# A 3x3 depthwise convolution as matmuls: its taps in 64-row or 64-column tiles, two halves of the tokens side by side

## Chip, core and metric

One core of a Trainium2 chip runs the whole program in one launch. The metric is the time of one execution on the device, in microseconds (us). About 0.2% of this kernel's time, 38 us, is what a measurement can tell from no change.

## What is computed

The input is four images of 64x64 tokens with 96 channels, in float32. Four layers are applied one after the other. Each layer adds a token mixer and then a feed-forward network (with 8-bit and 16-bit rounding) to the tokens. The mixer of layer 0 is a gated linear recurrence along the tokens. The mixers of layers 1 to 3 are two-dimensional selective scans over 192 inner channels. Ahead of each scan stands a depthwise 3x3 convolution, the part that is changed here:

```python
xz = x @ in_proj_w.T
xi, z = jnp.split(xz, 2, axis=-1)
xc = jnp.transpose(xi, (0, 3, 1, 2))
xc = jax.lax.conv_general_dilated(xc, conv_w, (1, 1), 'SAME', feature_group_count=Di) + conv_b[None, :, None, None]
xc = jax.nn.silu(xc)
```

Depthwise means that each of the 192 channels (`Di`) is convolved with nine weights of its own. The result `u` then runs through four directional scans of 4096 steps with 16 states for each channel.

## The kernel before

**Stages.** `gated` (line 1034) does layer 0 for the four images. Its work comes in 384 tiles of 512 tokens (4 images, 8 strips of 512 tokens, 12 groups of states). For each tile TensorE (PE) makes two projections into the wide PSUM tile `bc` and one into `c`. VectorE (DVE) turns them into a decay `da` and an input, and runs the recurrence as one scan instruction into `h`. GpSimd (POOL) multiplies `h` by `c`, and every third tile PE adds three products up into `sum`. `scans` (line 839) then does the twelve selective scans (three layers, four images) as 4608 tiles of 1024 tokens, 384 for each stage. In each tile ScalarE (ACT) computes `da`, PE broadcasts a row into the wide PSUM tile `bc` (`b_rows`, line 883), DVE multiplies (`bc<-du,bc`) and scans (`h<-da,carry,bc`), POOL multiplies by `c`, and PE adds the result into `acc` (`add_quarters`, line 919). `add_quarters` already issues its matmuls as four tiles of 64 rows by 64 columns, with `tile_position`.

**Between the stages.** All that lies between two scans of one image is written as Python generators: the previous mixer's end, the feed-forward network, the next layer's input projection and the convolution (`between`, line 623). A `Job` (line 717) advances them. It earns a number of steps with every tile (1.6 during the scans, 2.6 in layer 0 and for the last images), and at each step every live generator goes on to its next `yield`. So the number of `yield`s in a generator sets over how many tiles its work is spread. The convolution of image 0 ahead of layer 1 runs while layer 0 works on the images after it. The eleven others run during the scans.

**Order of the work.** `InOrder` (line 68) ties each engine's instructions to the order in which the program issues them. All of them are issued through one helper line, so the profile calls nearly every instruction L78, and groups are told apart by their tiles. On PE the order within a tile of the scans is the broadcast for the next tile, then the job's matmuls, then the accumulation of a tile that was scanned earlier. A matmul of the job thus stands ahead of the next broadcast.

**PSUM.** Two banks of 512 float32 columns serve all the job's matmuls (`x_proj`, `dt_proj`, `in_proj`, `conv` and others). `bank` (line 125) takes one and `release` gives it back at the end of the tile. `yield True` lets a generator go on only when a bank is free.

**The convolution.** `project_in` (line 511) leaves a strip of 8 image rows by 64 with a border in the SBUF tiles `pad0` and `pad1`. `pad0` holds channels 0 to 127. `pad1` holds channels 128 to 191 twice, in its upper 64 partitions shifted by one image row. `convolve` (line 570) multiplies shifted views of these by diagonal matrices, one for each tap, which `derive_taps` (line 300) makes once for each layer: nine of 128x128 for `pad0` (`tap_lo`) and six for `pad1` (`tap_hi`). The first three of the six handle two image rows at once over 128 partitions, and the last three use 64 partitions. Each group accumulates in one bank, which one ACT copy of 128x512 takes out to `u`. After that come the bias, the Silu and the stores. There are 96 strips in all (3 layers, 4 images, 8 strips), so 96 x 15 taps.

Of the kernel before, what the change touches and what calls it, by code (L numbers as in the profile page):

```python
# [14 lines left out]
AF = mybir.ActivationFunctionType  # L15
# [3 lines left out]
HW = 64  # L19
# [7 lines left out]
MM = 512  # L27
G = MM // 128
NSTRIP = L // MM
SR = MM // HW  # L30
# [12 lines left out]
W_CW = W_OUT + 2 * C  # L43
# [56 lines left out]
def metaformer(ctx: ExitStack, tc: tile.TileContext, x, l0_ab, l0_rest, ssm, ffn, out):  # L100
    nc = tc.nc
    pe, act, dve, pool, sp = (
        InOrder(tc, e) for e in (nc.tensor, nc.scalar, nc.vector, nc.gpsimd, nc.sync)
    )
# [6 lines left out]
    def sb(bufs, tag, shape, dtype=F32):  # L111
        return pools[bufs].tile(shape, dtype, tag=tag, name=tag)

    def const(name, shape, dtype=F32):
        return pools[1].tile(shape, dtype, name=name)
# [7 lines left out]
    banks = {"free": 2, "back": 0, "pool": pbc}  # L123

    def bank(name):
        banks["free"] -= 1
        return banks["pool"].tile([128, MM], F32, tag="ps", name=name)

    def release():
        banks["back"] += 1  # L130
# [28 lines left out]
    ident = const("ident", [128, 128])  # L159
    make_identity(nc, ident)  # L160
    twice = const("twice", [128, 128])
    for k in range(2):
        p = slice(64 * k, 64 * k + 64)
        dve.tensor_copy(twice[p, 0:64], ident[p, p])
        dve.tensor_copy(twice[p, 64:128], ident[p, p])
    stacked = twice[:, 0:64]
# [6 lines left out]
    for n in range(NS):  # L173
        for k in range(2):
            at = NS * k + n
# [101 lines left out]
    class Weights:  # L277
# [22 lines left out]
        def derive_taps(self, some):  # L300

            if 0 in some:
                self.lo = sb(1, "tap_lo", [128, 9, 128])
                self.hi = sb(1, "tap_hi", [128, 6, 128])
            for t in some:
                src, dst = (ident, self.lo[:, t, :]) if t < 9 else (twice, self.hi[:, t - 9, :])
                act.activation(dst, src, AF.Copy, scale=self.w[:, W_CW + t : W_CW + t + 1])

    weights = {}

# [109 lines left out]
    def measure_x(im, s, hold):  # L420

        x1 = load_x(im, s)
        yield
        yield
        norm = Norm()
        yield from norm.measure(x1, C, 1e-5)
        hold["x", s] = x1, norm
# [131 lines left out]
    def gate_z(im, s, hold):  # L559
        if s < NSTRIP:  # L560
            for z in hold["z"][s]:
                act.activation(z, z, AF.Silu)
# [7 lines left out]
    def convolve(im, layer, s, hold):  # L570

        lo, hi = hold["pads"].pop(s)
        taps = weights[layer]
        w = taps.w
        raw = []
        groups = (
            [(taps.lo[:, t, :], lo[:, t // 3 : t // 3 + SR, t % 3 : t % 3 + HW]) for t in range(9)],
            [(taps.hi[:, t, :], hi[:, 0:SR, t : t + HW]) for t in range(3)]
            + [(taps.hi[0:64, 3 + t, :], hi[0:64, 2 : 2 + SR, t : t + HW]) for t in range(3)],
        )  # L580
        for i, group in enumerate(groups):
            ps = bank("conv")
            for at, (lhs, rhs) in enumerate(group):
                pe.matmul(ps, lhs, rhs, start=at == 0, stop=at == len(group) - 1)
                yield
            v = sb(1, f"u{i}", [128, MM])
            act.copy(v, ps)
            release()
            yield i == 0
            raw.append(v)  # L590
        for i, v in enumerate(raw):
            act.activation(v, v, AF.Silu, bias=w[:, W_CB + i : W_CB + i + 1])
        gate_z(im, s + 1, hold)
        yield
        yield
        store_z(im, s + 1, hold)
        t = slice(s * MM, (s + 1) * MM)
        cols_a, part_c = hold["cols"]
        sp.dma_start(out=im.u[0, 0:64, t], in_=raw[0][0:64])
        sp.dma_start(out=im.u[1, 0:64, t], in_=raw[0][64:128])  # L600
        sp.dma_start(out=im.u[2, 0:64, t], in_=raw[1][0:64])
        for p, src, dst, c0, nc_ in (
            (slice(0, 128), raw[0], cols_a, 0, HW),
            (slice(0, 64), raw[1], part_c, 0, HW // 2),
            (slice(64, 128), raw[1], part_c, HW // 2, HW // 2),
        ):
            pool.tensor_copy(
                dst[p].rearrange("p (c r) -> p r c", r=HW)[:, SR * s : SR * s + SR, :],
                src[p].rearrange("p (r c) -> p r c", c=HW)[:, :, c0 : c0 + nc_],
            )  # L610
            if p.start or p.stop == 128:
                yield
        if s == NSTRIP - 1:
            yield
            sp.dma_start(out=im.u[1, 64:128, :], in_=cols_a[0:64])
            sp.dma_start(out=im.u[0, 64:128, :], in_=cols_a[64:128])
            for k in range(2):
                sp.dma_start(
                    out=im.u[2, 64:128, k * L // 2 : (k + 1) * L // 2],
                    in_=part_c[64 * k : 64 * k + 64],  # L620
                )

    def between(im, layer, dst=None):


        hold = {"in": {}, "pads": {}, "z": {}}
        new = dram.tile([L, C], F32, tag="x", name="x") if dst is None else dst

        def columns():
            return sb(1, "cols_a", [128, L]), sb(1, "part_c", [128, L // 2])  # L630

        def first():
            if layer:
                cols_a, part_c = hold["cols"] = columns()
                sp.dma_start(out=cols_a[0:64], in_=im.y[1, 64:128, :])
                sp.dma_start(out=cols_a[64:128], in_=im.y[0, 64:128, :])
                for k in range(2):
                    sp.dma_start(
                        out=part_c[64 * k : 64 * k + 64],
                        in_=im.y[2, 64:128, k * L // 2 : (k + 1) * L // 2],  # L640
                    )
                load_y(im, 0, hold)
            for _ in range(9 if layer else 3):
                yield

        yield [Chain(first())]
        done = {"y": 0, "x": 0, "end": 0}

        def joins():
            for s in range(NSTRIP):  # L650
                yield lambda: done["x"] > s - 2
                yield True
                yield from join_orders(im, s, hold)
                done["y"] += 1

        def mixers():
            for s in range(NSTRIP):
                yield lambda: done["end"] > s - 2 and (
                    layer == 0 or (done["y"] > s and hold["y", s][1].known)
                )  # L660
                if layer:
                    yield from mixer_out(im, layer, s, hold)
                else:
                    yield from measure_x(im, s, hold)
                done["x"] += 1

        def feeds():
            for s in range(NSTRIP):
                yield lambda: done["x"] > s and hold["x", s][1].known
                yield from feed_forward(im, layer, s, hold, new)  # L670
                done["end"] += 1

        yield [Chain(f()) for f in (feeds, mixers, joins)[: 3 if layer else 2]]
        if dst is not None:
            return

        def second():
            if layer + 1 not in weights:
                weights[layer + 1] = Weights(layer + 1)
                for _ in range(4):  # L680
                    yield
                weights[layer + 1].derive()
                for t in range(0, 15, 3):
                    yield
                    weights[layer + 1].derive_taps(range(t, t + 3))
            im.x = new
            im.u = dram.tile([3, 128, L], F32, tag="u", name="u")
            im.z = dram.tile([DI, L], F32, tag="z", name="z")
            hold["cols"] = columns()
            hold["in"][0] = load_x(im, 0)  # L690
            yield
            yield

        yield [Chain(second())]
        done = {"in": 0, "out": 0}

        def takes():
            for s in range(NSTRIP):
                yield lambda: done["out"] > s - 3
                yield from take_in(im, layer + 1, s, hold)  # L700
                done["in"] += 1

        def convolves():
            yield lambda: done["in"] > 0
            gate_z(im, 0, hold)
            yield
            yield
            store_z(im, 0, hold)
            for s in range(NSTRIP):
                yield lambda: done["in"] > min(s + 1, NSTRIP - 1)  # L710
                yield True
                yield from convolve(im, layer + 1, s, hold)
                done["out"] += 1

        yield [Chain(f()) for f in (convolves, takes)]
# [557 lines left out]
    with tc.tile_pool(name="pbig", bufs=2, space=bass.MemoryType.PSUM) as wides_pool:  # L1273
# [5 lines left out]
        for at in range(len(stages)):  # L1279
            jobs.append([])  # L1280
            if at + 1 < len(stages):
                im, layer = stages[at + 1]
# [126 lines left out]
```

## Time and profile before

| what | us |
|---|---|
| median of 3 runs | 19235.74 |
| lowest and highest | 19232.23, 19267.89 |
| profiled execution, own time | 19244.18 |
| profiled execution, span from first to last instruction | 19242.4 |
| DVE busy in it | 17682.6 |
| PE busy in it | 15910.7 |
| POOL busy in it | 13533.8 |
| ACT busy in it | 11062.2 |

In the trace a float32 matmul is two PE instructions, each with a weight load: 1728 rows of `conv<-pad,tap_lo` are 96 x 9 taps, twice. PE rows include the time until a matmul's end, so consecutive rows overlap, and the distance from start to start tells what a matmul takes from PE. A DVE that is busy nearly all the time in a stretch sets the pace there, and the waits of DVE in that stretch tell what could be won. PEclk is the clock that PE was granted, as a share of the full one.

### The profile page before, as it was taken

To read this page: it belongs to the slowest core of one execution; us is meant where nothing else is said; L and a number is where in the kernel's file an instruction comes from. 1 tells how busy PE (TensorE), PEld (TensorE's weight loads), DVE (VectorE), ACT (ScalarE), POOL (GpSimd) and SP (SyncE) were. 2 spreads that over 40 slices of the span, in tenths; PEclk is the share of its full clock that TensorE was granted. 3 is DMA by queue.
4 is the path that set the end of the run, shared out by engine and by line. 5 is a ranking of instruction groups with operands and counts; after the bars stand their busy time and mean duration, and the time that the engine had idled before them with its cause. 6 is when DMAs were issued, how large, how long until landed. Compare 5 with 4: busy or idle time off the path is not lost.

```text
span 19242.4 us, 219783 instructions
## 1 busy us (share of the span) xinstructions
PE 15910.7 (83%) x69248; PEld 4675.9 (24%) x69248; DVE 17682.6 (92%) x13768; ACT 11062.2 (57%) x17831; POOL 13533.8 (70%) x9222
## 2 busy tenths in 40 slices
PE   8998787787787788788888788788888788788887
PEld 3332121121122222222222222222222222222323
DVE  6757999999999999999999999999999999999985
ACT  4544564555555665665665665665665665666664
POOL 3434777777777777777777777777777777777775
PEclk9998796786787797797797797797787787788775
DMA  2213666666676667667667677667676676676664
GB/s 52 51 45 93 167 189 170 167 187 171 167 194 176 171 186 185 172 186 183 171 187 182 174 191 182 170 187 187 168 192 180 171 192 179 170 198 176 168 180 115
DMA packets 1269846, 3192.04 MB, mean 166 GB/s; under 512 B 440336, under 2 KB 440560, under 8 KB 1262544
## 3 DMA queue, kind: packets, MB, share of 16 engines
q1 hardware_dynamic: 1268688, 3177.97, 62.7%
q8 instruction: 559, 9.16, 0.2%
q14 instruction: 599, 4.91, 0.1%
HBM read 2818.51 MB, written 308.28 MB: 162 GB/s over the span
## 4 chain that ended last, share of the span: by engine, by line
DVE 62%; PE 17%; ACT 10%; issue 4%; DMA 3%; POOL 3%; SPq 1%; DVEq 1%; POOLq 0%; ACTq 0%
DVE h L78 43%; DVE bc L78 16%; ACT da L78 5%; PE bc L78 4%; PE acc L78 4%; PE conv L78 2%; ACT L78 2%; DMA c<-cs 2%; POOL c L78 1%; PE dt_proj L78 1%; SPq L78 1%; DVE st L78 1%; PE y_t L78 1%; PE c L78 1%; POOL du L78 1%
## 5 line engine op out<-in xcount | busy, mean ns | idle before, releaser
L78 POOL TENSOR_TENSOR c<-h,c 128x1024 f32<-128x1024 f32 (+1 forms) x4992 | 11337.3, 2274 | 5052.2 <-DVE h L78 3027.9
L78 DVE TENSOR_TENSOR_SCAN h<-da,carry,bc 128x1024 f32<-128x1024 f32 x4608 | 10798.8, 2343 | 559.6 <-POOL c L78 53.5
L78 PE MATMUL acc<-c,twice 64*64 64x512 f32 x36864 | 6386.0, 770 | 35.5 <-POOL c L78 31.2
L78 ACT ACTIVATE da<-delta,decay 128x1024 f32<-128x1024 f32 x4608 | 5285.0, 1148 | 1687.0 <-DVE h L78 1680.0
L78 PE MATMUL bc<-bs,sel 96*128 96x512 bf16 x9216 | 3509.2, 470 | 2769.7 <-DVE h L78 2671.1
L78 DVE TENSOR_TENSOR bc<-du,bc 128x1024 f32<-128x1024 f32 x4608 | 5567.0, 1208 | 181.5 <-PE bc L78 170.8
L78 ACT COPY carry<-h 128x1 f32<-128x1 f32 x3456 | 652.8, 189 | 3929.1 <-DVE h L78 3924.3
L78 PEld LDWEIGHTS <-sel 96*128 96x128 bf16 x9216 | 563.8, 102 | 7896.7 <-DVE h L78 6245.7
L78 PEld LDWEIGHTS acc<-c,twice 64*64 64x64 f32 x36864 | 1149.8, 156 | 2898.8 <-issue 2020.8
L78 ACT ACT_TABLE_LOAD x1287 | 1651.2, 1283 | 37.7 <-DVE mv L78 19.8
L78 PE MATMUL conv<-pad,tap_lo 128*128 128x512 f32 x1728 | 918.7, 638 | 0.0
L78 PE MATMUL dt_proj<-rows,w 12*128 12x512 f32 x1152 | 841.3, 817 | 6.4 <-ACT delta L78 3.9
L78 ACT COPY y<-acc 128x1024 f32<-128x1024 f32 x288 | 291.6, 1012 | 808.6 <-PE acc L78 785.8
L78 PE MATMUL x_proj<-u,xp 128*108 128x512 f32 x1152 | 715.0, 739 | 20.2 <-DMA xp<-in_ssm 8.5
L78 POOL TENSOR_TENSOR du<-delta,u 128x1024 f32<-128x1024 f32 x288 | 678.9, 2357 | 1.5 <-issue 1.5
L78 ACT ACTIVATE c<-c,l_bias 128x512 f32<-128x512 f32 x384 | 263.4, 686 | 658.4 <-PE c L78 655.7
L78 PE MATMUL conv<-pad,tap_hi 128*128 128x512 f32 (+1 forms) x1152 | 606.8, 630 | 1.6 <-ACT u L78 1.6
L78 DVE TENSOR_TENSOR_SCAN h<-da,l_carry,bc 128x512 f32<-128x512 f32 x384 | 491.5, 1280 | 42.4 <-DVE bc L78 1.8
L78 PE MATMUL y_t<-ident,pad 128*128 128x128 f32 (+1 forms) x1536 | 389.2, 340 | 51.3 <-DMA pad<-y 40.6
L78 PE MATMUL bc<-rows,u 96*128 96x512 f32 x768 | 395.4, 640 | 41.6 <-DVE h L78 41.6
L78 PEld LDWEIGHTS conv<-pad,tap_lo 128*128 128x128 f32 x1728 | 339.7, 204 | 324.4 <-issue 255.1
L78 PE MATMUL bc<-xp,u 96*128 96x512 f32 x768 | 391.0, 634 | 24.2 <-DVE h L78 24.0
(143 smaller groups left out, 12353.1 us busy)
## 6 DMA issues: line engine op xcount, KB each, us to landing
c<-cs SPq DMA_DIRECT2D x9216, 256.0 KB, 4.2
u<-u SPq DMA_DIRECT2D x288, 512.0 KB, 6.7
y<-y SPq DMA_DIRECT2D x1152, 128.0 KB, 3.5
y<-y SPq DMA_DIRECT2D x144, 512.0 KB, 6.2
xr<-x SPq DMA_DIRECT2D x224, 192.0 KB, 5.0
u<-u SPq DMA_DIRECT2D x288, 128.0 KB, 3.9
pad<-y SPq DMA_DIRECT2D x288, 128.0 KB, 4.8
z<-zl SPq DMA_DIRECT2D x96, 256.0 KB, 4.5
```

What stands on the lines that cost most here:

```text
L78: ins = f(*a, **k).ins
```

## The change

The diagonal tap matrices become 64 columns wide (`stacked` holds two 64x64 identities, one above the other, so partition p holds its weight in column p mod 64), in one tile `taps` of 15.

For the first group, a tap becomes four matmuls of 64 rows by 64 columns over 256 tokens: `j` picks the upper or lower half of the channels, `k` the first or second half of the strip's tokens. The channel halves accumulate in two PSUM banks, and the token halves in the lower and upper 64 partitions of each. For the second group, a tap becomes two matmuls of 64 columns, one for each half of the tokens, in one bank. The first three use 128 rows, the last three 64.

Four ACT copies of 64x256 instead of one of 128x512 take each group out, and put the quarters where they belong in `u`. The generator yields after every second tap and once at the end of a group, where it yielded after every tap. Before a strip it waits until both banks are free, in one step where there were two.

```diff
@@ def derive_taps(self, some):
-                self.lo = sb(1, "tap_lo", [128, 9, 128])
-                self.hi = sb(1, "tap_hi", [128, 6, 128])
+                self.taps = sb(1, "taps", [128, 15, 64])
             for t in some:
-                src, dst = (ident, self.lo[:, t, :]) if t < 9 else (twice, self.hi[:, t - 9, :])
-                act.activation(dst, src, AF.Copy, scale=self.w[:, W_CW + t : W_CW + t + 1])
+                act.activation(
+                    self.taps[:, t, :], stacked, AF.Copy, scale=self.w[:, W_CW + t : W_CW + t + 1]
+                )
@@ def convolve(im, layer, s, hold):
-        for i, group in enumerate(groups):
-            ps = bank("conv")
-            for at, (lhs, rhs) in enumerate(group):
-                pe.matmul(ps, lhs, rhs, start=at == 0, stop=at == len(group) - 1)
-                yield
+        half = MM // 2
+
+        def rows(k, first):
+            return slice(first + SR // 2 * k, first + SR // 2 * (k + 1))
+
+        def tap_lo(ps, t):
+            for k in range(2):
+                for j in range(2):
+                    p = slice(64 * j, 64 * j + 64)
+                    pe.matmul(
+                        ps[j][64 * k : 64 * k + 64, 0:half],
+                        taps[p, t, :],
+                        lo[p, rows(k, t // 3), t % 3 : t % 3 + HW],
+                        start=t == 0,
+                        stop=t == 8,
+                        tile_position=(64 * j, 64 * k),
+                    )
+
+        def tap_hi(ps, t):
+            m, first = (128, 0) if t < 3 else (64, 2)
+            for k in range(2):
+                pe.matmul(
+                    ps[0][64 * k : 64 * k + 64, 0:half],
+                    taps[0:m, 9 + t, :],
+                    hi[0:m, rows(k, first), t % 3 : t % 3 + HW],
+                    start=t == 0,
+                    stop=t == 5,
+                    tile_position=(0, 64 * k),
+                )
+
+        for i, (tap, n) in enumerate(((tap_lo, 9), (tap_hi, 6))):
+            ps = [bank("conv") for _ in range(2 - i)]
+            for t in range(n):
+                tap(ps, t)
+                if t % 2:
+                    yield
+            yield
             v = sb(1, f"u{i}", [128, MM])
-            act.copy(v, ps)
-            release()
+            for j in range(2):
+                for k in range(2):
+                    act.copy(
+                        v[64 * j : 64 * j + 64, half * k : half * (k + 1)],
+                        ps[j if i == 0 else 0][64 * k : 64 * k + 64, 0:half],
+                    )
+            for _ in ps:
+                release()
             yield i == 0
...
@@ def convolves():
-                yield lambda: done["in"] > min(s + 1, NSTRIP - 1)
-                yield True
+                yield lambda: done["in"] > min(s + 1, NSTRIP - 1) and banks["free"] > 1
                 yield from convolve(im, layer + 1, s, hold)
```

More of the change, by code (lines that the diff above doesn't have):

```diff
@@ L572, in convolve @@
         lo, hi = hold["pads"].pop(s)
-        taps = weights[layer]
-        w = taps.w
+        w, taps = weights[layer].w, weights[layer].taps
         raw = []
[L576 to L580, printed above, removed]
-        for i, group in enumerate(groups):
-            ps = bank("conv")
-            for at, (lhs, rhs) in enumerate(group):
-                pe.matmul(ps, lhs, rhs, start=at == 0, stop=at == len(group) - 1)
-                yield
-            v = sb(1, f"u{i}", [128, MM])
-            act.copy(v, ps)
-            release()
+        half = MM // 2
```

## Prediction

> **What bounds the kernel now.** I first read the page's shares and slices, then the busy time in chosen windows, then what DVE waits for in them. The page:
>
> ```profile
> PE 15910.7 (83%) x69248; PEld 4675.9 (24%) x69248; DVE 17682.6 (92%) x13768; ACT 11062.2 (57%) x17831; POOL 13533.8 (70%) x9222
> ...
> DVE  6757999999999999999999999999999999999985
> ```
>
> DVE is at 0.9 or more from about 2400 us on, but not in the first five slices. There are two regimes, layer 0 and the scans. The windows view shows one line from layer 0 with feed-forward work beside it, one from layer 0 with the convolution, and one from a scan stage with the convolution (columns: window and length, then PE, PEld, DVE, ACT, POOL busy, PE clock, DMA).
>
> ```profile
> 345.00:830.00 485.00, 441.24 (x1289) 176.88 (x1290) 373.43 (x598) 257.29 (x566) 226.06 (x390) 0.95 0.21 51
> 939.00:1466.00 527.00, 487.58 (x1228) 191.57 (x1226) 287.79 (x376) 238.83 (x486) 180.21 (x330) 0.94 0.19 47
> 8244.00:8669.00 425.00, 378.13 (x1584) 107.30 (x1583) 406.66 (x239) 270.95 (x448) 317.22 (x205) 0.93 0.69 188
> ```
>
> In layer 0 with the convolution PE is busy 487.6 of 527 us (93%), DVE 55%, ACT 45%, POOL 34%: PE is the bound. In the scan stage DVE is busy 406.7 of 425 (96%). DVE's waits in the latter two windows:
>
> ```profile
> DVE da L78 <- PE bc L78: 116.0, 58, 5.3
> ```
>
> ```profile
> DVE bc L78 <- PE bc L78: 3.0, 3, 2.4
> ```
>
> So a shorter convolution is worth its full PE time in layer 0 (one of twelve convolutions of an image) and nearly nothing in the eleven others, where DVE waits 3.0 us for PE in 425. Over the eleven windows these waits are 3.7, 4.5, 5.0, 1.2, 3.0, 3.8, 0.7, 3.3, 0.4, 3.8 and 0.7: **30 us in all**.
>
> **The change part by part.**
>
> *Streaming.* What one tap takes from PE now is read from starts. In layer 0:
>
> ```profile
> 1100.07 1.91 PE L78 MATMUL conv<-pad,tap_lo 128*128 128x512 f32 x4
> ...
> 1101.81 1.88 PE L78 MATMUL bc<-rows,u 96*128 96x512 f32 x4
> 1103.53 1.02 PE L78 MATMUL c<-rows,u 96*128 96x512 f32 x2
> ```
>
> Four instructions lie 1.72 to 1.74 us apart, 0.43 us each, so a tap (two) is 0.86 us. Matmuls in four tiles of 64x64 are already in the trace:
>
> ```profile
> 17244.40 1.98 PE L78 MATMUL conv<-pad,tap_hi 64*128 64x512 f32 x4
> 17246.31 1.09 PE L78 MATMUL acc<-y,twice 64*64 64x512 f32 x8
> 17247.22 1.04 PE L78 MATMUL acc<-c,twice 64*64 64x512 f32 x8
> 17248.19 0.60 PE L78 MATMUL bc<-bs,sel 96*128 96x512 bf16 x2
> ```
>
> Eight of them, four matmuls, take 17247.22 - 17246.31 = 0.91 us, hardly more than two instructions of the full array. The four run side by side, with two banks and tile positions as in the change. A first-group tap is the same eight instructions over 256 columns: half, 0.43 us. That instructions or weight loads don't set a floor above it is shown by `y_t<-ident,part_c` (8 instructions of 64 columns): 151.9 us for 3072, 49 ns each, 8 x 49 = 0.40 us at worst, below 0.43. A second-group tap has two tiles of 64 columns over 256 tokens; its nearest row is `sum<-c,fold 128*32` (three column tiles, six instructions in some 0.86 us at 512 columns), so also half. The convolution's PE time is 918.7 + 606.8 = 1525 us on the page, 124 of it in layer 0 (14.77 and 109.18 in the windows of 500:1000 and 1000:1500). Half of it goes: **62 us in layer 0**, some 700 in the scans.
>
> *Changes of tile shape.* Above, four `conv` instructions take 1.91 us between `bc` and `acc`, against 1.74 in layer 0 among matmuls of full width: 0.17 us for a stretch between shapes. In layer 0 the neighbours are 96*128 and the stretches now cost nothing extra. In the changed program's order the convolution stands in 30 tiles of layer 0 (56 before), so 30 stretches x 0.2 to 0.3 us: **+8 us** (bounds 0 and 15). In the scans it stands between `bc` (96*128) and `acc` (64*64) already, and the first group now has `acc`'s shape; I take 0. The Trainium skill, "TensorEngine Tiling (Array Packing)", section Key Properties, says that a change of tiling mode drains TensorE. The 0.17 us agree, and it speaks against the change in layer 0; the page has no price, so the sum goes by the row.
>
> *Taking the banks out.* Two copies of 128x512 become eight of 64x256 for each strip. ACT's groups:
>
> ```profile
> L78 ACT COPY u<-conv 128x512 f32<-128x512 f32 x192 | 109.7, 571 | 50.5 <-PE conv L78 36.7 <-POOL c L78 9.4 <-issue 3.8
> L78 ACT COPY yt<-y_t 128x384 f32<-128x384 f32 x192 | 89.4, 466 | 132.4 <-PE y_t L78 131.2
> ```
>
> 128 columns are worth 0.105 us, so 256 columns are 0.466 - 0.105 = 0.36 us. Eight are 2.89 against 1.14: +1.75 us for a strip, 168 us of ACT time over 96 strips, in fours of 1.44 us. Queued behind them on ACT are the next `carry` and `da`. `da` is issued two tiles (7.2 us) ahead of its scan, and ACT is busy 271 of 425 us in the scan window, 1.3 us free in each tile of 3.6. So I cost it at nothing. In layer 0 the cover is ACT's 55% of idle time. The same page's section PSUM Bottleneck warns that tiling speeds up the matmuls but not the copies; the rows agree (2.5 times the ACT time), but they lie beside DVE or PE.
>
> *Banks and yields.* The first group holds both banks, so `dt_proj` and `x_proj` may have to wait for one. In the changed order all but a few `dt_proj` stand in the same tiles of their item, none later than the eighth of 16 (its result is needed at the next item), and layer 0's preparation ends by the eighth of twelve tiles, where it ended by the seventh. Cost 0. There are nine yields for 15 taps instead of 15. A step now carries two taps of 0.43 us where it carried one of 0.86: the PE load of a tile stays the same, and the convolution is over in half as many tiles (464 for 880 in the scans). The jobs end some ten tiles earlier, with 50 to 90 tiles of each stage free of them already: no gain. ACT's table loads go from 1287 to 1289 (2.6 us, hidden). `derive_taps` saves 45 x 0.05 us on ACT: nothing.
>
> *Scans.* Half of the 30 us of waits goes with half of the tiles, -15; eviction and bank waits may give some back. I take **-10** (bounds -30 and +30). POOL and DMA do the same work. What is late next is DVE itself.
>
> *The sum*, on the profiled execution's own 19244.2 us: -62 + 8 in layer 0, -10 in the scans = -64, so 19180. The median of the runs is 8.4 us under that execution: 19235.7 - 64 = **19172**.
>
> **Bounds for layer 0.** Upper: the tiles of the convolution's window take 527/96 = 5.49 us, those of 345:830 take 485/120 = 4.04. If half of this difference went, 96 x 1.45 / 2 = 70. Lower: if only half of PE's saving shows, because ACT, POOL and DVE in turn hold a tile back, (62 - 8)/2 = 27.
>
> **The rivals.**
>
> 1. *As forecast*: 19172, from 19115 (70 in layer 0, 30 in the scans, 20 for the spread of runs) to 19197 (-38). Chance 0.71.
> 2. *The pace of layer 0 passes to another chain.* There `POOL c <- ACT c` waits are long, and DVE waits for `sum`. Against it: the window without convolution has PE at 91% with tiles of 4.04 us, so PE sets the pace there as well. It would give -27 in layer 0 and 0 in the scans: 19209. Chance 0.17.
> 3. *The change doesn't do what it says*: the two column tiles of one row half don't stream side by side over short pieces, and a tap stays 0.86 us. For it: no 256-column piece is in the trace. Against: `acc` and `part_c`. It gives +8 in layer 0: 19244. Chance 0.04.
> 4. *Slower: the copies come to the path.* Place: ACT in the scans' convolution windows. Price: 88 strips x 1.75 = 154 us there, less 54 in layer 0: +100, 19336. It decides once ACT runs more than the 7.2 us behind that `da` has. Against it: DVE waits for `da` 0.5 us at most in any of the eleven windows. Chance 0.08.
>
> **How the numbers follow.** About 0.2%, 38 us, is what a measurement can tell from no change. Rival 1 lies beyond it: faster 0.71. Rivals 2 and 3 lie within: same 0.21. Rival 4: slower 0.08. The range for 8 in 10 takes in rival 1 and most of rival 2: 19115 to 19215.
>
> **What would show it.** In the profile after, the eight instructions of a first-group tap should take about 0.43 us from start to start of the next tap, with the `conv` groups about 760 us less busy on PE; the tiles of layer 0 with convolution should take some 4.9 us instead of 5.5, and layer 0 should end some 55 us earlier; the scan stages should keep 3.6 to 3.7 us a tile. I am wrong if `conv` matmuls of one tap don't start within some ns of each other, if DVE waits for `da` in the scans' convolution windows, if the granted clock there falls well below 0.92 and waits for `bc` grow, or if layer 0's tiles stay at 5.5 with PE less busy.

## The result and the profile after

The changed kernel takes **19337.01 us** (median of 4 runs, 19331.18 to 19363.0) against 19242.88 for the kernel before in the same series: a ratio of 1.0050, interval 1.0032 to 1.0067. It is 94 us slower, where 64 us faster was forecast. The profiled execution took 19363.0 us with a span of 19361.2; it was the slowest of the four, so its difference to the profile before, 119 us, is somewhat more than the medians'. The page after:

```profile
PE 15633.4 (81%) x75584; PEld 4650.2 (24%) x75584; DVE 17685.9 (91%) x13768; ACT 11253.3 (58%) x18409; POOL 13553.0 (70%) x9222
...
DVE  6757999999999999999999999999999999998995
...
L78 PE MATMUL conv<-pad,taps 64*64 64x256 f32 (+1 forms) x9216 | 838.5, 414 | 6.2 <-ACT zh L78 2.9
```

The convolution on PE fell from 1525 to 838.5 us, as it should. DVE is busy 17685.9 us, where it was 17682.6. So nothing was added to the engine that sets the end; the 119 us are **all idle time of DVE**. In the slices it shows only in two digits near the end (8995 for 9985). The windows view finds it. One window covers layer 0 with the convolution, one the stage that the prediction showed (there 8244 to 8669); the columns are those of the prediction:

```profile
939.00:1450.00 511.00, 450.92 (x1776) 183.85 (x1776) 294.82 (x385) 256.38 (x542) 184.64 (x340) 0.91 0.22 54
8268.00:8648.00 380.00, 311.01 (x1938) 95.13 (x1934) 354.69 (x207) 254.15 (x441) 279.69 (x179) 0.87 0.70 189
```

In the scan stage the convolution now spans 380 us instead of 425, but DVE is idle for 25.3 of them, where it was idle for 18.3 of 425. Over all eleven such windows DVE's idle time is 254 us after and 201 before, in shorter windows. What DVE waits for, over the whole span, before and then after (total, times, longest):

```profile
DVE bc L78 <- PE bc L78: 170.8, 136, 7.0
...
DVE rows L78 <- ACT bs L78: 21.1, 7, 13.8
```

```profile
DVE da L78 <- PE bc L78: 303.8, 163, 9.6
DVE bc L78 <- PE bc L78: 236.2, 209, 7.0
DVE h L78 <- POOL c L78: 73.5, 29, 11.7
DVE rows L78 <- ACT bs L78: 71.2, 23, 14.9
```

Sorted by where the waits stand, the two traces differ so: `rows` for `bs` +51 us, all in the scans' convolution windows; `bc` for `bc` +21 in these windows, +27 in the stretches of the scans ahead of them and +14 in the last stage; `h` for POOL's `c` +17 just after a convolution's end; layer 0 as a whole -16. Layer 0 ends 17.6 us earlier (1723.9 us for 1741.5), and all that follows it takes 136 us longer.

**Where the 51 us arise.** The wait of `rows` is new in these windows. It belongs to `x_proj`, the projection of the next item's tokens, which takes a bank from the same two as `conv` and `dt_proj`. A stretch of the timeline after (start, duration, engine, operation):

```profile
9925.77 1.88 PE L78 MATMUL x_proj<-u,xp 128*108 128x512 f32 x4
...
9927.59 1.88 PE L78 MATMUL conv<-pad,taps 128*64 128x256 f32 x14
...
9930.47 1.11 PE L78 MATMUL x_proj<-u,xp 128*108 128x512 f32 x2
...
9931.62 0.59 ACT L78 COPY rows<-x_proj 108x512 f32<-108x512 f32 x1 [5.07 <-PE x_proj L78]
9932.10 0.57 ACT L78 CAST bs<-x_proj 32x512 bf16<-32x512 f32 x1
9932.70 0.68 DVE L78 TENSOR_TENSOR rows<-x_proj,bs 32x512 f32<-32x512 f32 x1 [2.70 <-ACT bs L78]
```

The end of an `x_proj` group, its two ACT copies and DVE's subtraction follow each other with nothing between. DVE's instructions are in order, so the scan behind the subtraction waits too: 2.70 us. Such a place comes about when the item's preparation is not done in time: at the head of a chunk of the scans (line 1018 of the changed kernel) the program issues whatever of it is left at once, ahead of the tile's own work. Counted in the order of the instructions, **19 `x_proj` groups** are forced out there after the change (13 with a matmul, six with their two copies alone), and none before. That they were late because the convolution's first group held both banks is tested below.

### The profile page after: what moved, and what is told of

The parts are those of the page before. It is cut to its first block, busy times and chain, and to the rows that moved or that the text cites. A ratio compares the mean times of both kernels' runs of the same rounds, so it can differ in the third digit from the quotient of the medians.

```text
span 19361.2 us, 233014 instructions
## 1 busy us (share of the span) xinstructions
PE 15633.4 (81%) x75584; PEld 4650.2 (24%) x75584; DVE 17685.9 (91%) x13768; ACT 11253.3 (58%) x18409; POOL 13553.0 (70%) x9222
## 4 chain that ended last, share of the span: by engine, by line
DVE 45%; PE 11%; ACT 8%; DMA 3%; issue 3%; POOL 2%; SPq 0%; DVEq 0%; POOLq 0%; ACTq 0%
DVE h L78 31%; DVE bc L78 12%; ACT da L78 4%; PE acc L78 4%; PE bc L78 2%; DMA c<-cs 2%; ACT L78 1%; PE dt_proj L78 1%; PE y_t L78 1%; PE x_proj L78 1%; POOL c L78 1%; DVE st L78 1%; PE out_proj L78 1%; POOL du L78 1%; PE conv L78 1%
## 5 line engine op out<-in xcount | busy, mean ns | idle before, releaser
L78 PE MATMUL acc<-c,twice 64*64 64x512 f32 x36864 | 6560.3, 784 | 49.5 <-POOL c L78 49.5
L78 PE MATMUL bc<-bs,sel 96*128 96x512 bf16 x9216 | 3564.2, 477 | 3061.0 <-DVE h L78 2968.9
L78 PEld LDWEIGHTS acc<-c,twice 64*64 64x64 f32 x36864 | 1233.7, 159 | 2623.3 <-issue 1905.5
L78 PE MATMUL conv<-pad,taps 64*64 64x256 f32 (+1 forms) x9216 | 838.5, 414 | 6.2 <-ACT zh L78 2.9
L78 PE MATMUL x_proj<-u,xp 128*108 128x512 f32 x1152 | 754.3, 775 | 41.0 <-ACT pad L78 14.8
L78 PEld LDWEIGHTS conv<-pad,taps 64*64 64x64 f32 (+1 forms) x9216 | 400.8, 143 | 479.9 <-issue 300.8
L78 PE MATMUL out_proj<-w,u 128*128 128x96 f32 (+1 forms) x1536 | 389.5, 367 | 12.2 <-POOL u L78 11.9
```

Source lines behind the costliest of these rows:

```text
L78: ins = f(*a, **k).ins
```

## The experiments

In the expectations, theory A is that the second bank costs the time, theory B that the copies do, theory C that the denser yields do. Each ratio is to the kernel before in the same series, whose medians lie between 19246.9 and 19254.9 us. "The 96 tiles" are tiles 216 to 311 of layer 0, beside which the convolution runs, timed from scan to scan. There is one profile for each kernel, and in these the first 216 tiles of layer 0, which the edits leave all but alone, vary by up to 17 us.

**One part at a time.** To the kernel before, one part of the change is added: a second, unused bank; the four copies; the yields. To the kernel after, a rule is added that a strip's first group starts only when no preparation is under way.

```diff
 e2_two_banks (on before)
             ps = bank("conv")
+            spare = bank("spare") if i == 0 else None
...
             release()
+            if spare is not None:
+                release()
...
-                yield lambda: done["in"] > min(s + 1, NSTRIP - 1)
-                yield True
+                yield lambda: done["in"] > min(s + 1, NSTRIP - 1) and banks["free"] > 1
 e3_quarter_copies (on before)
-            act.copy(v, ps)
+            for j in range(2):
+                for k in range(2):
+                    p, c = slice(64 * j, 64 * j + 64), slice(MM // 2 * k, MM // 2 * (k + 1))
+                    act.copy(v[p, c], ps[p, c])
 e4_gate (on after)
-... and banks["free"] > 1
+... and banks["free"] > 1 and banks["quiet"]()
+        banks["quiet"] = lambda: segment is None or segment.done
 e5_pacing (on before)
                 pe.matmul(ps, lhs, rhs, start=at == 0, stop=at == len(group) - 1)
-                yield
+                if at % 2:
+                    yield
+            yield
```

> The kernel before, whose first group takes the second PSUM bank as well (and leaves it empty) and waits for both like the changed kernel. Matmuls, copies and yields are those of before. Theory A (the second bank is what costs: x_proj gets no bank, is forced out at the head of an item, and DVE waits in order behind it): in the program's order 28 x_proj groups stand late, against 19 in the changed kernel and none before, so DVE waits for bs in the scans' convolution windows of about 28 x 2.5 = 70 us, and 60 to 130 us slower than before in all. Theory B (the eight copies) and theory C (the denser yields): within 20 us of before, for neither is in it.

Measured: 19369.91 us, ratio 1.0062 (1.0046 to 1.0077). A bank that is held and never written costs by itself as much as the whole change: +119 us. DVE's waits in it:

```profile
DVE da L78 <- PE bc L78: 311.5, 172, 8.8
DVE bc L78 <- PE bc L78: 183.4, 155, 10.6
DVE rows L78 <- ACT bs L78: 119.4, 34, 14.9
DVE h L78 <- POOL c L78: 87.6, 30, 15.7
```

`rows` waits 119.4 us where it waited 21.1, and 28 `x_proj` groups are forced out. Theory A's mechanism is there, in its purest form. In layer 0 the same kernel is faster: the 96 tiles take 497.5 us for 527.5, with the same matmuls and the wait for both banks in one step (15 of the 1229 matmul instructions come just behind these tiles).

> The kernel before, with each group taken out by four copies of 64x256 instead of one of 128x512, and nothing else. Theory A (second bank) and theory C (yields): within 20 us of before. Theory B (the copies delay ACT's bs and da): 50 to 110 us slower, with DVE waits for bs as in the changed kernel.

Measured: 19285.33 us, ratio 1.0016 (1.0006 to 1.0025), +31 us, between what theory B and the others gave. The wait for `bs` stays at 24.2 us. The cost sits in `bc` for `bc` (+20 in the convolution windows) and in layer 0 (+16 in all; the 96 tiles take 540.5 us for 527.5). The copies cost something, but a third of the change.

> The changed kernel, whose first group starts only when no segment is being prepared (x_proj never waits for it); in the program's order no x_proj group stands late. Theory A (second bank): the waits for bs in the convolution windows go, 60 to 110 us faster than the changed kernel, so 10 to 50 us faster than before, by the gain of layer 0. Theories B (copies) and C (denser yields): within 25 us of the changed kernel, some 90 us slower than before.

Measured: 19273.45 us, ratio 1.0014 (1.0004 to 1.0023). No `x_proj` group is late, and 0.36 of the changed kernel's 0.50% are gone. But theory A alone said 10 to 50 us faster than before, and that failed. Something else eats the gain of the shorter matmuls.

> The kernel before, with a yield after every second tap and one at the end of a group, as in the changed kernel, but with its own matmuls, one bank and one copy. A step then carries two taps of 0.86 us, twice the PE load of either kernel. Theory C (density costs): slower than before by at least the 95 us of the changed kernel. Theory A (second bank) alone: within 30 us of before, unless PE itself gets late, which would show as DVE waits for bc and not for bs.

Measured: 19498.33 us, ratio 1.0128 (1.0112 to 1.0145). With matmuls of full length, two taps to a step cost 250 us:

```profile
DVE bc L78 <- PE bc L78: 453.3, 308, 19.8
```

453.3 us for 170.8: +204 of it stands in the convolution windows, and a further 58 after the convolution's end, mostly as a single wait in the same tile of the stages (below). This is the price of doubling a tile's job work. In the change each tap is half as long, so the run only shows that the yields are not free.

**What the halved matmuls are worth alone.** Four kernels. `h1_half_taps` computes the taps over the first 256 tokens of a strip only, and one copy writes them twice. It thus **leaves out the convolution of the second half of the tokens**, and so do `h2`, `h3` and `h4` below. Each tap takes PE half as long (the convolution's rows fall from 1525 to 913 us); banks, number of copies, order and yields stay those of before. `p1_dense_layer0` has the matmuls of before and yields after every second tap in layer 0 alone. `e6_slow_pacing` is after with a yield after each tap. `e1_second_group` puts only the second group in column tiles, which needs one bank.

```diff
 h1_half_taps (on before)
-                pe.matmul(ps, lhs, rhs, start=at == 0, stop=at == len(group) - 1)
+                pe.matmul(
+                    ps[:, 0 : MM // 2], lhs, rhs[:, 0 : SR // 2], start=at == 0, stop=at == len(group) - 1
+                )
...
-            act.copy(v, ps)
+            act.copy(
+                v.rearrange("p (k t) -> p k t", k=2),
+                ps[:, None, 0 : MM // 2].to_broadcast([128, 2, MM // 2]),
+            )
 p1_dense_layer0 (on before; "dense" is true in layer 0)
-                yield
+                if at % 2 or not banks["dense"]:
+                    yield
+            if banks["dense"]:
+                yield
 e6_slow_pacing (on after)
-                if t % 2:
-                    yield
-            yield
+                yield
 e1_second_group (on before; tap_hi as in the change, four copies for it)
-            for at, (lhs, rhs) in enumerate(group):
-                pe.matmul(ps, lhs, rhs, start=at == 0, stop=at == len(group) - 1)
+            for t in range(n):
+                tap(ps, t)
                 yield
```

> The kernel before, but each tap runs over the first 256 tokens of a strip only and the one copy writes them twice: the convolution of the second half of the tokens is left out. Order, yields, banks and copies are those of before, and PE loses half of the convolution's time (some 760 us, 62 us of it in layer 0). It measures by itself what the halved matmul time is worth. As predicted (PE bounds layer 0 there): layer 0's window of tiles 216 to 312 falls by 55 to 65 us, 60 to 80 us faster in all. Rival (layer 0 is held by round trips between the engines, and PE's rows overstate its load): 10 to 30 us in that window, 15 to 45 us in all.

Measured: 19200.02 us, ratio 0.9973 (0.9962 to 0.9983). **-52 us is what half of the convolution's PE time is worth** at the yields of before, with nothing paid for it; it lies between what the two theories gave. The 96 tiles take 500.9 us for 527.5: -27, not 55 to 65. Layer 0 ends 11 us earlier (in this execution its first, unchanged part took 8 us longer). In the scans' convolution windows DVE is idle for 179 us instead of 201: -22, not -10.

> The kernel before, with a yield after every second tap and one at a group's end in layer 0 alone; full matmuls, one bank, one copy. If PE bounds layer 0: 0 within 10 us there, for PE's work is the same. If the steps of the job do (each round trip lies on the tile's path, and fewer steps mean fewer loaded tiles): 20 to 35 us faster in layer 0 and in all.

Measured: 19220.93 us, ratio 0.9986 (0.9977 to 0.9994). Its PE work is that of before, to the instruction. The 96 tiles take 495.2 us for 527.5, and layer 0 ends 17 us earlier (here the first 216 tiles took 16 us longer). The windows view of the 96 tiles, in the columns of the prediction: the kernel before, `p1`, `h1`, then `h2` (below; half taps with the yields of the change) and the changed kernel.

```profile
938.82:1466.33 527.51, 487.76 (x1229) 191.62 (x1227) 288.19 (x377) 239.16 (x488) 180.61 (x330) 0.94 0.19 47
954.38:1449.56 495.18, 473.16 (x1229) 187.28 (x1227) 286.28 (x377) 233.85 (x484) 180.50 (x330) 0.97 0.23 55
946.30:1447.22 500.92, 446.66 (x1227) 196.06 (x1225) 287.59 (x376) 238.55 (x489) 181.40 (x331) 0.91 0.20 50
954.66:1434.71 480.05, 441.23 (x1227) 193.29 (x1225) 286.46 (x377) 233.73 (x484) 180.56 (x330) 0.93 0.23 57
939.82:1441.73 501.91, 443.43 (x1746) 181.00 (x1738) 287.30 (x376) 249.70 (x531) 180.71 (x330) 0.91 0.22 55
```

The same 1229 matmul instructions went through in 32 us less, so the amount of PE's work alone did not set the pace. Of the 32, 18 are less idle time of PE, and 15 less busy time at a higher granted clock. Half of the work is worth 27 us at the yields of before (`h1`) and 15 at the denser ones (`p1` to `h2`). So both count, how many tiles carry job work and how much each carries, and neither gives the 62 us.

> The changed kernel with a yield after every tap, so that its program order on PE is that of the kernel before with two banks held (28 late x_proj groups), but with taps of half the time and eight copies. Against that kernel (119 us slower than before): if the halved matmul time is worth little and the copies cost some 35 us, about 100 to 150 us slower than before; if the halved time is what was forecast, at most 60 us slower.

Measured: 19383.47 us, ratio 1.0069 (1.0055 to 1.0082), about that of the unused bank (1.0062). With a yield after each tap the two banks are held for nine steps instead of five, 28 `x_proj` groups are late, and the waits of `rows` for `bs` grow to 135.9 us. In layer 0 the halved matmuls do show (the 96 tiles take 477.5 us, for 497.5 in `e2`), but not in the whole.

> The kernel before, with the second group alone in column tiles of 64 (two halves of the tokens side by side, four copies); the first group, the yields and one bank for each group as before. Copies at half the price of the run with quarter copies: +10 to +20 us. Halved time of six of fifteen taps: -5 to -25 us. In all within 25 us of before, and no DVE waits for bs in the convolution windows.

Measured: 19226.31 us, ratio 0.9987 (0.9978 to 0.9996). The part of the change that needs one bank and keeps the yields gains 25 us, its copies included. No wait for `bs` comes with it.

**Building the change up from `h1`.** `h2_half_dense` is `h1` with the yields of the change; `h3_half_two_banks` is `h2` with the second bank held and waited for. What separates `h3` from the changed kernel is the copies and the tile shapes. `b1` and `b2` try versions: `b1` is `e1` and `p1` together; `b2` is `e1` with the first group in four tiles of 64x64 and two banks in layer 0 only, where no `x_proj` wants a bank, with a yield after each tap.

```diff
 h2_half_dense (on h1)
-                yield
+                if at % 2:
+                    yield
+            yield
 h3_half_two_banks (on h2): the edit of e2
 b2_first_layer (on e1)
-        for i, (tap, n) in enumerate(((tap_lo, 9), (tap_hi, 6))):
-            ps = bank("conv")
+        quarters = banks["first"]
+        for i, (tap, n) in enumerate(((tap_quarters if quarters else tap_lo, 9), (tap_hi, 6))):
+            both = quarters and i == 0
+            ps = [bank("conv") for _ in range(2)] if both else bank("conv")
```

> The kernel before with taps over half the tokens (the convolution of the second half is left out) and the changed kernel's yields; one bank, one copy. Against the run with half taps alone (ratio 0.9973) it measures the denser yields by themselves at the halved PE time. If denser yields cost little (each tile's PE load is that of before): 0.996 to 0.999, layer 0 some 15 us better. If they are what keeps the gated version above before: 1.000 to 1.002, with DVE waits for bc in the scans' convolution windows.

Measured: 19293.77 us, ratio 1.0025 (1.0015 to 1.0035): +0.52% over `h1` from the yields alone, though the 96 tiles of layer 0 take only 480.0 us. Some 70 us of it have one place: in tile 313 of eight stages DVE waits 6 to 9 us (20 in one stage) for `bc`. The timeline of `h2` there:

```profile
10047.89 4.90 SPq L78 DMA_DIRECT2D u<-part_c  x2
...
10064.54 1.44 SPq L78 DMA_DIRECT2D u<-u  x3
...
10071.40 2.04 PE L78 MATMUL x_proj<-u,xp 128*108 128x512 f32 x2 [8.42 <-DMA u<-u]
...
10078.46 1.23 DVE L78 TENSOR_TENSOR bc<-du,bc 128x1024 f32<-128x1024 f32 x1 [8.41 <-PE bc L78]
```

The convolution ends with large stores of `u` (first line). Some 17 us later the next item loads its `u` on the same queue (second line). PE stands at `x_proj` for 8.42 us until they land, the broadcast of the next tile is behind it on PE, and DVE waits 8.41 us. Before, the convolution ended some twenty tiles later, and its stores did not stand ahead of these loads. What is late is mostly the loads' issue: in `h4` (below), with the stores put off, those of this stage are issued 12 us earlier in their item. They land 7 to 11 us after their issue here, and 5 to 7 there.

> The same with the second bank held by the first group: the program order is that of the changed kernel, 19 late x_proj groups, but one copy of full width and half the tokens left out. If the bank is the greater part of the changed kernel's loss: 50 to 80 us above the run without it, with DVE waits for bs of 40 to 60 us. The changed kernel's 1.005 less this one is then the price of the eight copies and of the tile shapes: 20 to 50 us.

Measured: 19332.2 us, ratio 1.0039 (1.0026 to 1.0051). `rows` for `bs` goes up by 57 us, with 19 late groups as in the changed kernel. But the convolution is now stopped while it waits for both banks and ends some twelve tiles later, so the waits of tile 313 go (-70 us). The net is 38 us, +0.14%, which is within the intervals and below the 50 to 80 expected.

> The kernel before with the second group in column tiles, and in layer 0 a yield after every second tap. The two single runs gave 0.9987 and 0.9986, about 25 us each; if they add, 0.997 to 0.998, 40 to 55 us faster than before.

Measured: 19214.13 us, ratio 0.9981 (0.9972 to 0.9990), less than the sum of its parts (-0.13% and -0.14%) but within the intervals of it.

> The second group in column tiles everywhere; the first group in 64x64 tiles with two banks only in layer 0, where no x_proj waits for a bank, with a yield after every tap as in the run that ended layer 0 32 us earlier. In the scans the first group is that of before. If the loss is the bank in the scans: 45 to 65 us faster than before (0.9965 to 0.9977). If the two banks or the copies cost in layer 0 too: within 30 us of before.

Measured: 19202.4 us, ratio **0.9974** (0.9964 to 0.9985). This beats both kernels, by 0.26% and by 0.76%. Its 96 tiles take 484.2 us, with the two banks held there. It gets as much as `h1` did, with the whole convolution computed, but some half of that can hang on where the convolution ends (`b3` below).

**Whether the end's stores are the other half.** The four large stores at a convolution's end are put off by eleven more yields: in `h2` (`h4`), in the changed kernel (`x2`), in `e4` (`x3`) and in `b2` (`b3`).

```diff
         if s == NSTRIP - 1:
-            yield
+            for _ in range(12):
+                yield
```

> The run with half taps and the changed kernel's yields (1.0025, half the tokens' convolution left out), with the four large stores at the end of a convolution put off by eleven more yields. There one DVE wait of 6 to 9 us for bc at tile 313 of eight stages, 20 us in one, where x_proj waits for u behind those stores. If that coincidence makes the greater part of the denser yields' cost: 60 to 80 us less, 0.998 to 0.9995, and no such wait. If density itself is the cost: no more than 20 us less.

Measured: 19250.98 us, ratio 0.9999 (0.9990 to 1.0008), 0.26% less than `h2`; the waits of tile 313 are gone (DVE for `bc` after the convolution's end: 78 us in `h2`, 7 here). What is left over `h1`, another 0.26%, goes with the density itself: waits for `bc` in the convolution windows grow by 53 us, from 10 to 63. One place of it in the timeline of `h4`, at the start of an item:

```profile
9826.72 2.07 PE L78 MATMUL dt_proj<-rows,w 12*128 12x512 f32 x2
...
9828.72 3.78 PE L78 MATMUL conv<-pad,tap_lo 128*128 128x256 f32 x8
...
9834.43 1.89 PE L78 MATMUL conv<-pad,tap_lo 128*128 128x256 f32 x8
9834.63 1.23 DVE L78 TENSOR_TENSOR bc<-du,bc 128x1024 f32<-128x1024 f32 x1 [1.30 <-PE bc L78]
```

A `dt_proj` and four taps stand in one tile, and the same eight instructions that take 1.89 us one tile later take 3.78 here: the windows view gives a granted clock of 0.50 from 9827 to 9832 us and 1.00 from 9834 to 9837. Together they run past the 3.6 us of a tile, and DVE waits 1.30 us. At the full clock the two would have taken about half of their 5.85 us (an estimate from these rows), so this wait takes both, the fuller tile and the low clock.

> The changed kernel with the same four stores put off by eleven yields. Its own waits of DVE for POOL's c and for bc after the convolution's end sum to some 40 us over before. If those come from the stores meeting the rows of c and the loads of layer 0: 20 to 45 us less than the changed kernel, 1.0025 to 1.004. The waits for bs (bank) and those inside the convolution's windows stay.

Measured: 19303.85 us, ratio 1.0029 (1.0019 to 1.0039): 0.21% less than the changed kernel, as expected; the waits for `bs` stay. 30 us of it can be pointed at. The waits for POOL's `c` after a convolution's end go down by 16. So does one wait of layer 0 by 14, which is this one in the changed kernel:

```profile
1376.27 4.88 SPq L78 DMA_DIRECT2D u<-part_c  x2
1381.20 2.60 SPq L78 DMA_DIRECT2D x<-in_x  x1
...
1392.02 0.74 DVE L78 BATCH_NORM_STATS2 st<-x 128x6 f32<-128x96 f32 x4 [15.68 <-DMA x<-in_x]
```

The convolution's large stores were issued just ahead of the next strip's load of `x`, and DVE waited 15.68 us for it. It landed 10.8 us after its issue, where the median of the 32 such loads is 2.8. In `x2` the 96 tiles take 484.4 us for the changed kernel's 501.9. In the kernel before, the convolution ended in another tile.

> The changed kernel with both repairs: the first group starts only when no segment is being prepared, and the large stores at the end come eleven yields later. Matmuls in tiles, eight copies and denser yields stay. If bank and stores are separate and add: 1.005 - 0.0036 - 0.0021, about 0.999 to 1.000. If the gate had already moved the stores out of the way in the scans, only layer 0's wait for x is left: 1.0005 to 1.0014.

Measured: 19285.46 us, ratio 1.0015 (1.0006 to 1.0024), the same as `e4`. The gate had already moved the stores in the scans. Layer 0's wait for `x` goes (the 96 tiles take 484.6 us for 501.3 in `e4`), but the whole does not get faster, so these 17 us are lost again behind layer 0: DVE's waits in the scans ahead of the convolutions are 21 us longer than in `e4` and those in the last stage 14, two places whose cause stays open (below).

> The fastest kernel so far (second group in column tiles, first group in tiles only in layer 0; 0.9974) with the large stores put off by eleven yields. In the kernel before few waits follow the convolution's end, so 0 to 20 us less: 0.9965 to 0.9975.

Measured: 19233.84 us, ratio 0.9989 (0.9981 to 0.9998), worse than `b2` by 0.15%, just beyond the intervals. Where the end of a job lands costs here what it saves elsewhere; later is not better by rule.

**The ledger**: halved matmuls -0.27% (`h1`, uncertain by 0.1%); the end's stores ahead of loads +0.26% (`h2` less `h4`); density +0.26% (`h4` less `h1`); the second bank +0.14% net (`h3` less `h2`; +0.62% where it stands alone, `e2`); copies and shapes +0.11% (after less `h3`; +0.16% in `e3`). The differences are each uncertain by 0.13 to 0.2%. The sum is +0.50%, the measured change. The terms are differences along one chain of kernels, so this sum had to come out, and another order shares it out otherwise: at the denser yields the same half of the taps is worth 1.03% (`e5` less `h2`), and the yields ahead of it cost 1.28% (`e5`). On the changed kernel itself the gate takes off 0.36%, late stores 0.21%, both together 0.35%. Two runs outside the chain support it: `e3` prices the copies near the chain's value, and `e4`, which has the changed kernel's matmuls, copies and yields without the late groups and, in the scans, without the early stores, came to 1.0014, where `h4` and the copies give 1.0010 to 1.0015.

## Why the prediction was wrong, point by point

**The streaming was right.** In the changed kernel's timeline four taps of the first group lie between these starts:

```profile
9772.44 1.96 PE L78 MATMUL conv<-pad,taps 64*64 64x256 f32 x32
9774.22 1.04 PE L78 MATMUL acc<-c,twice 64*64 64x512 f32 x8
```

(9774.22 - 9772.44) / 4 = 0.445 us a tap, against 0.43 forecast, and the groups are 687 us less busy on PE, against 760. Rival 3 falls. Two small readings were off, and nothing hung on them: six instructions of `sum` take 0.99 us and not some 0.86, and the slices show DVE below 0.9 in the first four and the last two, not in the first five.

**The first step that failed is that in layer 0 a shorter convolution is worth its full PE time, because "PE is the bound".** It came from PE's 93% in the window of layer 0, with rows that overlap, as the section on the profile says itself. The -62 was -27 in `h1`, which was the lower bound and rival 2's figure, and -15 at denser yields. The five lines above show where it went in `h1`. PE's busy time times the granted clock, its work at the full clock, fell by some 52 us (458 to 406). But the clock fell as well, so PE was busy for only 41 us less, and its idle time grew by 14.5. In the changed kernel the 96 tiles took 26 us less, and 43 without the wait behind its own stores (`x2`), of 54 forecast; a part of this is luck, since `e2`, `e5` and `p1` gained 29 to 32 us there without any shorter matmul. The +8 for changes of shape was not measured alone; `x2` and `h4`, which differ in layer 0 by shapes, copies and the second bank, take 484.4 and 483.1 us. The Trainium skill, "Trainium Kernel Development and Optimization", section Performance Expectations, calls matmul busy time a bad metric for how close a kernel is to roofline, since matmuls are pipelined. The lines agree: PE is 92% busy before, and 96% with the same work in `p1`.

**The greater part of the miss lies behind layer 0**: 136 us longer in the profile, where 10 shorter was forecast. Most of it comes from three terms that were put at nothing.

**"Banks: cost 0" failed.** The working looked at the order of `dt_proj` and never at that of `x_proj`, which takes a bank from the same two. 19 of its groups became late, and the waits of `rows` for `bs` are 2 to 5 us each. Layer 0 has no `x_proj`, and there two banks cost nothing that shows (`e2`, `b2`). The Trainium skill, "TensorEngine Tiling (Array Packing)", section Gotcha 1: PSUM Pressure, says that row tiles write to different PSUM banks and so press on PSUM. `e2` shows its price here, +119 us, and that it falls not on the convolution but on the other users of the banks.

**"Yields: the PE load of a tile stays the same" failed.** Twice over: a step also does what other generators do in that tile (`dt_proj`, `x_proj`), so halving the steps makes fuller tiles (+0.26%); and the convolution ends elsewhere, where its stores stand ahead of loads that are needed soon (+0.26% in `h2`, 0.21% in the changed kernel by `x2`). The prediction did see that the jobs end some ten tiles earlier and took that for harmless. It costed the DMAs that move with them at nothing, without looking at what is next on SP's queue.

**"Copies: hidden" was wrong by some 20 to 31 us.** The duration was right (279.8 / 768 = 0.364 us, forecast 0.36). But they are not hidden. In `e3` PE waits longer for ACT to free a bank (`z` 13.3 to 18.2, `conv` 1.6 to 5.7, `dt_proj` 3.9 to 5.5 us), with the next `bc` behind it; that is some 11 of the 20 us by which `bc` came later there. The rest is not traced.

**"Scans -10" was too small** for the halved matmuls, which alone give -22 there (`h1`).

**Rival 4** gave 19336 and the result is 19337, but for another reason: the agreement is luck. Its mark, waits of DVE for `da` in the scans, did not come: `h` waits for `da` 6.3 us in the whole span. The copies cost about a quarter of its price; the bank and the yields make up the rest.

Of the signs given, the two that said "wrong" were there: the clock in the scans' convolution windows fell from 0.91-0.94 to 0.85-0.88, and waits for `bc` grew. But the clock alone does not explain the loss: in `h1` it fell to 0.87 to 0.90 as well, and that kernel is faster; in `e2` it stayed at 0.92 to 0.95, and that one is 119 us slower.

**What stays open.** The +27 us of `bc` waits in the scans ahead of the convolutions and part of the last stage's +14 arise where the program's order is the same in both kernels. They may be the spread between two profiled executions, or a shift that earlier delays carry along; no run separates these, though in `x2`, with the same order there, the first of the two is +4. Nor is it settled why a loaded tile of layer 0 costs what it does: `p1` and `e2` exclude PE's amount of work alone, and `p1` had a higher granted clock as well.

## What to carry to other kernels

- Before paying for a shorter step, measure what its time is worth by itself: leave half of the work out and keep all else. Here 613 us of PE's rows were worth 52. Do it at the pacing of both versions: with the denser yields the same half was worth 1.03%, some 200 us (`e5` to `h2`).
- Count every user of a shared pool (here two PSUM banks) in the order of the instructions, not the one that seems nearest. A pool that is held longer shows as lateness of the others, far from the change.
- A generator's yields set where its end lands, and its stores with it. Look at what is queued behind them, and at the fullest tile rather than the mean one.

## What the runs showed of the hardware

- Four 64x64 tiles over 256 columns run side by side: most of the starts within a stretch are 6 to 7 ns apart, eight instructions take 0.445 us, and half-length pieces keep the gain that full-length ones had (0.91 us for 512 columns).
- With less matmul work the granted clock was lower here: in the scans' convolution windows 0.91 to 0.94 before, 0.87 to 0.90 with half of the taps (`h1`), 0.85 to 0.88 after the change. In the 96 tiles of layer 0 PE's busy time times the clock agrees for the same work (458 and 459 us, before and `p1`; 406 and 410, `h1` and `h2`), so a lower clock gives back part of what is saved.
- At a granted clock of 0.50 the eight instructions of four halved taps took 3.78 us, and 1.89 at 1.00 (`h4`).
- Large stores just ahead on the same queue made loads late in two ways: in `h2` the loads of `u` were issued 12 us later (PE waited 8.42 us), and after the change a load of `x` landed after 10.8 us instead of 2.8 (DVE waited 15.68 us).
